# A mixture-of-experts stage: the first expert's first block placed ahead of the turning of the remaining rows

## The chip, the cores and the metric

The kernel runs on one core of one Trainium2 chip. The metric is the device time of one execution in microseconds (us); beside it stands a profile of one execution, taken by the hardware profiler. The engines are named as the profile names them: PE is TensorE (matmuls), PEld its weight loads, DVE is VectorE, ACT is ScalarE, POOL is GpSimd, SP is SyncE, which here only starts DMAs. A name with a q (PEldq, POOLq) is the engine's sequencer, which takes instructions, branches and register loads in order.

## The reference

Two layers of a graph network with attention over 1250 nodes of 512 features (float32), and at the end of the second layer a mixture of eight experts. Only this last part is touched:

```python
def _L1_ffn_ref(x, ln_g, ln_b, w_r, b_r, W1, b1, W2, b2):   # E=8, K=2, 512 -> 2048 -> 512
    h = (x - mu) * jax.lax.rsqrt(var + LN_EPS) * ln_g + ln_b
    logits = jnp.einsum('btd,ed->bte', h, w_r) + b_r
    topk_vals, topk_idx = jax.lax.top_k(logits, K)
    gates = jax.nn.softmax(topk_vals, axis=-1)
    hid = jax.nn.gelu(jnp.einsum('nd,edf->nef', hf, W1) + b1, approximate=False)
    expert_stack = jnp.einsum('nef,efd->ned', hid, W2) + b2
    ...
    mixed = jnp.sum(gathered * gates_flat[:, :, None], axis=1)
    return x + mixed
```

The reference runs every expert on every row and then picks two results per row. The kernel sends each row only to its two experts.

## The kernel before, in words

**Routing and sorting.** The stages ahead of the experts (layer norms, graph sums, attention) work on ten tiles of 125 rows. They leave the normalized rows in DRAM (`rows_d`), and for each row its two experts and its two gates. The 2 x 1250 (row, expert) pairs are sorted by expert into 2500 *slots*: VectorE makes one-hot matrices and TensorE adds them up. The helper `listed` (from line 1157) does this: it makes `blk`, `nblk`, `inb`, then `hotp` and `hotb` for each of the two choices on VectorE, then 20 matmuls into `plist` (line 1179). It is called twice. The first call gives `row_i`, the row of each slot, in 20 *blocks* of 128 slots. The second one gives the lists `to_row` and `to_gate`, the target row and gate of each slot of each block of results; its last copies are lines 1246 to 1254. Between them lie the plan (lines 1203 to 1219) and the gates (from line 1222). The plan has four whole numbers for each expert: its first slot, its number of full blocks of 256, whether what is left of it needs 0, 128 or 192 slots (0, 1 or 2), and its first column in the lists.

**Gathering and turning.** The loop of lines 1191 to 1200 runs over the 20 blocks. GpSimd gathers 128 rows by an indirect DMA (line 1193) into one of five tiles `hg`; TensorE turns the tile by four transposes (line 1197) into a PSUM tile `pg`, of which there are four; `affine_columns` (lines 154 to 163) brings each of the four pieces into `hts`, the rows' features by slots, with scale and shift on the way. VectorE does two of the pieces, ScalarE the other two. `hts` lies in SBUF as a whole.

**Experts.** The loop at the end (lines 1334 to 1346) runs over the eight experts with branches on the plan. First comes what is left over, at one of two widths: `If part > 0` (line 1341), in it `If part == 1` (line 1342), a block of 128, or else of 192. Then `blocks_of_256` (line 1320) follows: up to four ifs, one nested in the other (line 1322), each with a block of 256. A `block` (line 1311) calls `hidden` (line 1260): for each of 16 chunks of the 2048 hidden features four matmuls (line 1266) and one GELU on ScalarE (line 1269). Then `result` (line 1281) has 16 matmuls and one for the bias for each 128 slots (lines 1287 and 1289), and `add_rows` (line 1271) scales by the gate on VectorE (line 1278) and adds the rows to the output in DRAM by an indirect DMA of GpSimd (line 1279). For 192 slots `result_192` (line 1292) does the same turned, with transposes at the end. `plan_of` (line 1326) loads the four numbers of an expert into registers of each engine (line 1328), one expert ahead. With these inputs expert 0 has one block of 128, expert 1 one of 192, expert 2 one of 128; the other five together have four of the small ones and seven of 256.

**Weights.** Each expert has eight tiles of 1 MB (four of W1, four of W2), and 16 places hold two experts. `load_weights` (line 1084) issues them from SP in order, up to a given number. Places 0 to 7 have a pool of their own. Places 8, 9 and 10 lie in `big`, an old buffer of the stages ahead, and places 11 to 15 in a pool `moe_w2` that takes the room of the sorting pools `rt` and `rx`, once nothing uses them any more.

**Order.** Each engine executes its own queue in order. The tile framework's scheduler sets that order by the program's order and the dependences; on SP inside the expert loop the order is that of the program (`manual_schedule`). Between engines semaphores make an instruction wait for its inputs and for the room that it writes.

Of the kernel before, what the change touches and what calls it, by code (L numbers as in the profile page):

```python
# [8 lines left out]
F32 = mybir.dt.float32  # L9
# [10 lines left out]
N = 1250  # L20
# [27 lines left out]
NA_B = (2 * N + E1 * 127) // 128  # L48
WS = 16
# [20 lines left out]
def gps_two_layer_kernel(ctx: ExitStack, tc: tile.TileContext, x, src, dst, ew, rows, cols,  # L70
# [1034 lines left out]
    with tc.tile_pool(name="moe", bufs=1) as ep:  # L1105
# [4 lines left out]
        with tc.tile_pool(name="rt", bufs=1) as rt, tc.tile_pool(name="rx", bufs=3) as rx, \  # L1110
                tc.tile_pool(name="rps", bufs=2, space=PSUM) as ps:
            iota_p = rt.tile([P, 128], F32, name="iota_p")
            nc.gpsimd.iota(iota_p, pattern=[[1, 128]], base=0, channel_multiplier=0,
                           allow_small_or_imprecise_dtypes=True)
            edges_b = rt.tile([P, NB], F32, name="edges_b")
            nc.gpsimd.iota(edges_b, pattern=[[128, NB]], base=0, channel_multiplier=0,
                           allow_small_or_imprecise_dtypes=True)

            tok = rt.tile([P, T, 2], F32, name="tok")
            nc.gpsimd.iota(tok[:, :, 0], pattern=[[0, T]], base=0, channel_multiplier=1,  # L1120
                           allow_small_or_imprecise_dtypes=True)
            nc.gpsimd.iota(tok[:, :, 1], pattern=[[1, T]], base=0, channel_multiplier=0,
                           allow_small_or_imprecise_dtypes=True)
            edges_a = rt.tile([P, NA_B], F32, name="edges_a")
            nc.gpsimd.iota(edges_a, pattern=[[128, NA_B]], base=0, channel_multiplier=0,
                           allow_small_or_imprecise_dtypes=True)
            steps = rt.tile([P, MB], F32, name="steps")
            nc.gpsimd.iota(steps, pattern=[[256, MB]], base=193, channel_multiplier=0,
                           allow_small_or_imprecise_dtypes=True)
            nc.vector.memset(hts[:, :, NB * 128:], 0.0)  # L1130


            prank = ps.tile([P, T, E1], F32, name="prank", tag="pl")
            flat = "p t e -> p (t e)"
            nc.tensor.matmul(prank.rearrange(flat), lower, has.rearrange(flat), start=True, stop=False)
            nc.tensor.matmul(prank.rearrange(flat), ones_b, before[:, :T, :].rearrange(flat), start=False, stop=True)
            pbase = ps.tile([P, E1], F32, name="pbase", tag="pt")
            nc.tensor.matmul(pbase, ones_b, below, start=True, stop=True)
            pcount = ps.tile([P, E1], F32, name="pcount", tag="pt")
            nc.tensor.matmul(pcount, ones_b, before[:, T, :], start=True, stop=True)  # L1140
            base = rt.tile([P, E1], F32, name="base")
            nc.vector.tensor_copy(base, pbase)
            count = rt.tile([P, E1], F32, name="count")
            nc.vector.tensor_copy(count, pcount)


            rank = rt.tile([P, T, E1], F32, name="rank")
            nc.vector.tensor_tensor(rank, prank, base[:, None, :].to_broadcast([P, T, E1]), ALU.add)
            def of_expert(by, name):

                w = rt.tile([P, T, 2, E1], F32, name="hotw", tag="hotw")
                nc.vector.tensor_tensor(w, hot, by, ALU.mult)
                o = rt.tile([P, T, 2], F32, name=name)
                nc.vector.tensor_reduce(o, w, AX.X, ALU.add)
                return o

            def listed(slot, edges, nb, values, nv):

                blk = rt.tile([P, T, 2, nb], F32, name="blk", tag="blk")
                nc.vector.tensor_tensor(blk, slot[:, :, :, None].to_broadcast([P, T, 2, nb]),  # L1160
                                        edges[:, None, None, :].to_broadcast([P, T, 2, nb]), ALU.is_ge)
                nblk = rt.tile([P, T, 2], F32, name="nblk", tag="nblk")
                nc.vector.tensor_reduce(nblk, blk, AX.X, ALU.add)
                inb = rt.tile([P, T, 2], F32, name="inb", tag="inb")
                nc.vector.scalar_tensor_tensor(inb, nblk, -128.0, slot, op0=ALU.mult, op1=ALU.add)
                nc.vector.tensor_scalar(inb, inb, 128.0, None, op0=ALU.add)
                nc.vector.tensor_sub(blk[:, :, :, :nb - 1], blk[:, :, :, :nb - 1], blk[:, :, :, 1:])
                hotp = rt.tile([P, T, 2, 128], BF16, name="hotp", tag="hotp")
                hotb = rt.tile([P, T, 2, nv, nb], BF16, name="hotb", tag=f"hotb{nv}")
                for k in range(2):  # L1170
                    nc.vector.tensor_tensor(hotp[:, :, k, :], inb[:, :, k:k + 1].to_broadcast([P, T, 128]),
                                            iota_p[:, None, :].to_broadcast([P, T, 128]), ALU.is_equal)
                    nc.vector.tensor_tensor(hotb[:, :, k, :, :],
                                            blk[:, :, k, None, :].to_broadcast([P, T, nv, nb]),
                                            values(k)[:, :, :, None].to_broadcast([P, T, nv, nb]), ALU.mult)
                pl = ps.tile([128, nv, nb], F32, name="plist", tag="pl")
                for t in range(T):
                    for k in range(2):
                        nc.tensor.matmul(pl.rearrange("p m b -> p (m b)"), hotp[:, t, k, :],
                                         hotb[:, t, k, :, :].rearrange("p m b -> p (m b)"),  # L1180
                                         start=(t == 0 and k == 0), stop=(t == T - 1 and k == 1))
                return pl

            slot = of_expert(rank[:, :, None, :].to_broadcast([P, T, 2, E1]), "slot")
            plist = listed(slot, edges_b, NB, lambda k: tok, 2)
            row = rt.tile([128, NB], F32, name="row")
            nc.vector.tensor_scalar(row, plist[:, 1, :], float(P), None, op0=ALU.mult)
            nc.vector.tensor_add(row, row, plist[:, 0, :])
            row_i = rt.tile([128, NB], I32, name="row_i")
            nc.vector.tensor_copy(row_i, row)  # L1190
            for b in range(NB):
                hg = rx.tile([128, D], F32, name="hg", bufs=5)
                nc.gpsimd.indirect_dma_start(hg, None, rows_d,
                                             bass.IndirectOffsetOnAxis(ap=row_i[:, b:b + 1], axis=0))
                pt = ps.tile([128, DC, 128], F32, name="pg", tag="pg", bufs=4)
                for c in range(DC):
                    nc.tensor.transpose(pt[:, c, :], hg[:, c * 128:(c + 1) * 128], ident)
                affine_columns(hts[:, :, b * 128:(b + 1) * 128], pt, C_LNG, C_LNB)
# [3 lines left out]
            n256 = rt.tile([P, E1, MB], F32, name="n256")  # L1202
            nc.vector.tensor_tensor(n256, count[:, :, None].to_broadcast([P, E1, MB]),
                                    steps[:, None, :].to_broadcast([P, E1, MB]), ALU.is_ge)
            planf = rt.tile([P, 4, E1], F32, name="planf")
            nc.vector.tensor_copy(planf[:, 0, :], base)
            nc.vector.tensor_reduce(planf[:, 1, :], n256, AX.X, ALU.add)
            nc.vector.scalar_tensor_tensor(planf[:, 2, :], planf[:, 1, :], -256.0, count,
                                           op0=ALU.mult, op1=ALU.add)
            over = rt.tile([P, E1], F32, name="over")  # L1210
            nc.vector.tensor_scalar(over, planf[:, 2, :], 128.0, None, op0=ALU.is_gt)
            nc.vector.scalar_tensor_tensor(planf[:, 2, :], planf[:, 2, :], 0.0, over, op0=ALU.is_gt, op1=ALU.add)
            blocks_of = rt.tile([P, E1], F32, name="blocks_of")
            nc.vector.scalar_tensor_tensor(blocks_of, planf[:, 1, :], 2.0, planf[:, 2, :],
                                           op0=ALU.mult, op1=ALU.add)
            nc.vector.memset(planf[:, 3, 0:1], 0.0)
            for e in range(1, E1):
                nc.vector.tensor_add(planf[:, 3, e:e + 1], planf[:, 3, e - 1:e], blocks_of[:, e - 1:e])
# [175 lines left out]
```

## Time and profile before

| | |
|---|---|
| runs | 1548.17, 1550.3, 1555.47 us; median 1550.3 |
| the profiled execution | 1546.89 us; its span in the profile 1545.2 us, mean clock of TensorE 0.962 |
| TensorE | 5762 matmuls, transposes among them |
| the gathers (line 1193) | 20, starting from 811.3 to 841.2 us |
| result matmuls of line 1287 | 576, 592 ns each |
| hidden matmuls of line 1266 | 1792; 336 to 357 ns each by group |
| weights | 64 tiles of 1024 KB |

The span is what the profile covers from the first to the last instruction; the execution's own time is 1.7 us longer. All positions are us from the start of the span. The expert stage takes the second half, from about 803 us. A line of instructions is read as: start, busy time, engine, line, operation, output <- input, tile and shape, how many, and in brackets the idle time of the engine ahead of it and what ended that. "issue" as a cause of idle time means that the engine waited for nothing that the profile shows; the time then lies in its sequencer. The granted clock is the share of full speed that TensorE's throttle allowed.

### The profile page before, as it was taken

How to read it: one execution, taken by the hardware profiler on the slowest of the kernel's cores; microseconds unless marked ns; L12 is line 12 of the kernel's file. 1: busy time of each engine (PE TensorE's matmuls, PEld its weight loads, DVE VectorE, ACT ScalarE, POOL GpSimd, SP SyncE). 2: the span in 40 equal slices, each digit the busy share in tenths (PEclk: the TensorE clock that was granted, in tenths of full speed). 3: DMA queues.
4: the chain of work that ended last, by engine and by line, in shares of the span. 5: the costliest groups of instructions: out<-in, count | busy, mean ns of one | idle time of the engine just before them, and what ended most of it. 6: DMA issues, size and time to landing. Idle time of an engine off the chain costs nothing. (4 is left out here: it accounts for less than half of the span.)

```text
span 1545.2 us, 17805 instructions
## 1 busy us (share of the span) xinstructions
PE 1424.8 (92%) x5762; PEld 917.7 (59%) x5762; DVE 576.3 (37%) x1424; ACT 405.5 (26%) x937; POOL 95.2 (6%) x90
## 2 busy tenths in 40 slices
PE   6999999999999789999965898898999998899997
PEld 3666666634464436564544596794767567875773
DVE  7767666698876673343476000000000000000000
ACT  9544444400133413111224121210212012120110
POOL 0001100100000000000005000000000000000000
PEclk9999999999999899999985999899999999999999
DMA  7311111442420040001148556600642106000011
GB/s 226 94 53 54 48 54 41 139 129 74 147 75 21 1 157 3 0 0 33 48 154 334 175 187 231 221 9 12 223 139 95 14 8 226 12 6 9 7 14 15
DMA packets 72716, 134.73 MB, mean 87 GB/s; under 512 B 8281, under 2 KB 9673, under 8 KB 72575
## 3 DMA queue, kind: packets, MB, share of 16 engines
q1 hardware_dynamic: 67646, 122.47, 23.5%
q0 software_dynamic: 4928, 10.43, 3.5%
q8 instruction: 82, 1.34, 0.4%
q14 instruction: 60, 0.48, 0.1%
HBM read 107.27 MB, written 26.38 MB: 86 GB/s over the span
## 5 line engine op out<-in xcount | busy, mean ns | idle before, releaser
L1287 PE MATMUL po<-w,big 128*128 128x512 f32 x576 | 250.1, 592 | 0.0
L1266 PE MATMUL pm<-hts,big 128*128 x960 | 186.5, 357 | 21.8 <-issue 21.6
L1266 PEld LDWEIGHTS pm<-hts,big 128*128 128x128 f32 x960 | 168.6, 197 | 41.8 <-issue 26.3
L1278 DVE TENSOR_SCALAR o<-po,to_gate 128x512 f32<-128x512 f32 (+1 forms) x24 | 17.7, 748 | 459.6 <-PE po L1289 458.4
L1287 PEld LDWEIGHTS po<-w,big 128*128 128x128 f32 x576 | 109.1, 190 | 132.1 <-issue 131.5
L1269 ACT ACTIVATE big<-pm,cols_sb 128x256 f32<-128x256 f32 (+2 forms) x224 | 96.4, 432 | 282.2 <-PE pm L1266 281.9
L412 PEld LDWEIGHTS pa<-hm,hs 125*128 125x128 f32 x640 | 106.8, 189 | 95.9 <-issue 69.2
L1266 PE MATMUL pm<-hts,w 128*128 x832 | 144.5, 336 | 18.9 <-DMA big<-in_w_dram 6.0
L1266 PEld LDWEIGHTS pm<-hts,w 128*128 128x128 f32 x832 | 132.9, 197 | 29.8 <-issue 20.6
L412 PE MATMUL pa<-hm,hs 125*128 125x160 f32 x640 | 121.2, 301 | 8.4 <-DVE at L415 7.5
L415 DVE TENSOR_TENSOR at<-at,pa 128x160 f32 x320 | 102.2, 320 | 56.6 <-PE pa L412 33.6
L441 PE MATMUL pm<-big,ht 128*125 128x512 f32 x240 | 123.0, 597 | 0.0
L122 PE MATMUL pm<-w,at 128*125 128x512 f32 x240 | 114.2, 598 | 0.0
L388 ACT ACTIVATE hm<-hm,wt_e 125x80 f32<-125x80 f32 x320 | 86.5, 350 | 84.7 <-DVE hm L385 68.5
L619 PE MATMUL pn<-big,at 125*125 125x512 f32 x200 | 87.8, 596 | 2.1 <-DMA bg_sb<-in_rows_dram 2.1
L441 PE MATMUL pm<-big,xt 128*125 128x512 f32 x160 | 83.8, 612 | 1.2 <-ACT xt L275 1.2
L1269 ACT ACT_TABLE_LOAD x11 | 14.1, 1283 | 267.0 <-PE pm L1266 267.0
L1279 POOL DMA_INDIRECT out_dram<-o,row x24 | 36.9, 1536 | 660.4 <-DVE o L1278 284.4
L619 PEld LDWEIGHTS pn<-big,at 125*125 125x125 f32 x200 | 36.9, 188 | 50.6 <-issue 50.6
L1300 PE MATMUL po<-big,w 128*128 128x192 f32 x384 | 63.9, 327 | 0.0
L1300 PEld LDWEIGHTS po<-big,w 128*128 128x128 f32 x384 | 62.3, 190 | 0.6
L122 PEld LDWEIGHTS pm<-w,at 128*125 128x125 f32 x240 | 41.3, 188 | 34.7 <-issue 34.3
(382 smaller groups left out, 1444.5 us busy)
## 6 DMA issues: line engine op xcount, KB each, us to landing
w<-in_w_dram SPq DMA_DIRECT2D x52, 1024.0 KB
big<-in_w_dram SPq DMA_DIRECT2D x12, 1024.0 KB
x_t<-in_x_dram SPq DMA_DIRECT2D x10, 224.0 KB
xn_d<-xr SPq DMA_DIRECT2D x10, 224.0 KB
y_d<-o SPq DMA_DIRECT2D x10, 224.0 KB
z_d<-o SPq DMA_DIRECT2D x10, 224.0 KB
q_d<-o SPq DMA_DIRECT2D x10, 224.0 KB
k_d<-o SPq DMA_DIRECT2D x10, 224.0 KB
```

The source lines that it names most:

```text
L122: nc.tensor.matmul(ps, lhs[:, c, :], w[:, c, :], start=(c == 0), stop=(row is None and c == DC - 1))
L388: nc.scalar.activation(hm[:, j, 1, :], hm[:, j, 0, :], AF.Copy, scale=wt_e[:, g * J + j:g * J + j + 1])
L412: nc.tensor.matmul(pa.rearrange("p k c -> p (k c)"), hs[:, j, :], hm[:, j, :, :].rearrange("p k c -> p (k c)"), start=True, stop=True)
L415: add = nc.vector.tensor_tensor(to, to, pa.rearrange("p k (t w) -> p k t w", t=T), ALU.add)
L441: nc.tensor.matmul(pm, lhs[:, c, :], w_sb[:, c, :], start=(c == 0), stop=(row is None and c == DC - 1))
L619: nc.tensor.matmul(pn, at[:P, 0, s, t * P:(t + 1) * P], y[:, s, :], start=(s == 0), stop=(s == T - 1))
L1266: nc.tensor.matmul(pm[:, :width], w1s[e, f // DC][:, c, (f % DC) * 128:(f % DC + 1) * 128], hts[:, c, bass.ds(start, width)], start=(c == ...
L1269: nc.scalar.activation(hid[f][:, :width], pm[:, :width], AF.Gelu, bias=cols_sb[:, C_B11 + e * FC + f:C_B11 + e * FC + f + 1])
L1278: nc.vector.tensor_scalar(o[:n], pm[:n], to_gate[:n, here], None, op0=ALU.mult)
L1279: nc.gpsimd.indirect_dma_start(out, bass.IndirectOffsetOnAxis(ap=row[:n], axis=0), o[:n], None, bounds_check=N - 1, oob_is_err=False, comp ...
L1287: nc.tensor.matmul(pm, hid[f][:, s * 128:(s + 1) * 128], w2s[e, f // DC][:, f % DC, :], start=(f == 0), stop=False)
L1300: nc.tensor.matmul(pm[:, :192], w2s[e, f // DC][:, f % DC, chunk], hid[f][:, :192], start=(f == 0), stop=False)
```

## The change

The pieces of the stage are put in another order:

- The plan and both lists (gates too) are made ahead of any turning in the program's text; only the first `HG` = 10 gathers stand ahead of them.
- There are ten tiles `hg` in place of five. They move to the pool `rt`, which stays open until the last row is turned.
- Blocks 0 and 1 of the gathered rows are turned, in PSUM tiles `pg`, and then expert 0's first block runs at once. Its first slot is the constant 0 in place of a register. It is 256 wide if the expert has a full block of 256, or else its leftover at 128 or 192.
- Blocks 2 to 19 are turned behind that block, in the PSUM pool of the results (`po`, four tiles in place of three), with the gathers of blocks 10 to 19 among them, each in the text ahead of the turning of the block eight places before it.
- A new number `left_0` is made on VectorE (three small instructions): expert 0's leftover where it has a full block, else 0. After the turning it is loaded into a register, and the loop over the experts begins for expert 0 with it: its leftover and then its full blocks from the second on. With these inputs both are empty.
- Places 8, 9 and 10 of the weights are asked for by a `load_weights(WS_B)` of their own ahead of the first block. Places 11 to 15 follow, as before, once the sorting pool is closed, which is now behind the turning.

In the instruction order that results, SP issues places 8 and 9 in the routing stage (after the output of its tiles 3 and 7) and 10 ahead of the plan. GpSimd issues twelve gathers, then the row addition of the first block, and then the other eight gathers. TensorE has the list matmuls of the first call, the transposes of blocks 0 and 1, those of the second call, the first block, and then 72 transposes.

```diff
-        with tc.tile_pool(name="rt", bufs=1) as rt, tc.tile_pool(name="rx", bufs=3) as rx, \
-                tc.tile_pool(name="rps", bufs=2, space=PSUM) as ps:
+        left_0 = ep.tile([1, 1], I32, name="left_0")
+        sorting, sums = ExitStack(), ExitStack()
+        rt = sorting.enter_context(tc.tile_pool(name="rt", bufs=1))
+        ps = sums.enter_context(tc.tile_pool(name="rps", bufs=2, space=PSUM))
...
-            for b in range(NB):
-                hg = rx.tile([128, D], F32, name="hg", bufs=5)
-                nc.gpsimd.indirect_dma_start(hg, None, rows_d,
-                                             bass.IndirectOffsetOnAxis(ap=row_i[:, b:b + 1], axis=0))
-                pt = ps.tile([128, DC, 128], F32, name="pg", tag="pg", bufs=4)
-                for c in range(DC):
-                    nc.tensor.transpose(pt[:, c, :], hg[:, c * 128:(c + 1) * 128], ident)
-                affine_columns(hts[:, :, b * 128:(b + 1) * 128], pt, C_LNG, C_LNB)
+        def gather(b):
+            rows_at[b] = rt.tile([128, D], F32, name="hg", bufs=HG)
+            nc.gpsimd.indirect_dma_start(rows_at[b], None, rows_d,
+                                         bass.IndirectOffsetOnAxis(ap=row_i[:, b:b + 1], axis=0))
+        def turn_block(b, psum, **kw):
+            pt = psum.tile([128, DC, 128], F32, **kw)
+            hg = rows_at.pop(b)
+            for c in range(DC):
+                nc.tensor.transpose(pt[:, c, :], hg[:, c * 128:(c + 1) * 128], ident)
+            affine_columns(hts[:, :, b * 128:(b + 1) * 128], pt, C_LNG, C_LNB)
+        for b in range(HG):
+            gather(b)
...
+        nc.vector.tensor_scalar(over[:, 0:1], planf[:, 1, 0:1], 0.0, None, op0=ALU.is_gt)
+        nc.vector.tensor_mul(planf[:, 2, 1:2], planf[:, 2, 0:1], over[:, 0:1])
+        nc.vector.tensor_copy(left_0, planf[0:1, 2, 1:2])
...
+        for b in range(2):
+            turn_block(b, ps, name="pg", tag="pg", bufs=4)
+        sums.close()
+        load_weights(WS_B)
...
             def block(e, plan_e, b, width):
-                start = nc.s_assert_within(first + b * 256, 0, 2 * N - 1, ...)
+                start = 0 if e == 0 and isinstance(b, int) and b == 0 else nc.s_assert_within(...)
...
+            def rest_of(e, plan_e, part, b):
+                with tc.If(part > 0):
+                    with tc.If(part == 1) as one:
+                        block(e, plan_e, b, 128)
+                    with one.Else():
+                        block(e, plan_e, b, 192)
...
-                plans = {0: plan_of(0)}
+                plan_0 = plan_of(0)
+                with tc.If(plan_0[1] > 0) as full_0:
+                    block(0, plan_0, 0, 256)
+                with full_0.Else():
+                    rest_of(0, plan_0, plan_0[2], 0)
+                for b in range(2, NB):
+                    if b + HG - 2 < NB:
+                        gather(b + HG - 2)
+                    turn_block(b, po, name="po")
+                sorting.close()
+                w_pools[1] = ctx.enter_context(tc.tile_pool(name="moe_w2", ...))
+                _, (part_0,) = nc.values_load_multi_w_load_instructions(left_0, min_val=0, max_val=2, ...)
                 for e in range(E1):
                     load_weights(2 * FG * (e + 2))
-                    plan_e = plans.pop(e)
+                    plan_e = plans.pop(e) if e else plan_0
                     if e + 1 < E1:
                         plans[e + 1] = plan_of(e + 1)
-                    with tc.If(plan_e[2] > 0):
-                        with tc.If(plan_e[2] == 1) as one:
-                            block(e, plan_e, plan_e[1], 128)
-                        with one.Else():
-                            block(e, plan_e, plan_e[1], 192)
-                    blocks_of_256(e, plan_e, 0)
+                    rest_of(e, plan_e, plan_e[2] if e else part_0, plan_e[1])
+                    blocks_of_256(e, plan_e, 0 if e else 1)
```

## The prediction

> **What bounds the kernel now.** I read the page first, then the stretch of the trace around the change, since the page averages over very different stages.
>
> ```profile
> PE 1424.8 (92%) x5762; PEld 917.7 (59%) x5762; DVE 576.3 (37%) x1424; ACT 405.5 (26%) x937; POOL 95.2 (6%) x90
> issue 7%; PE 5%; DMA 1%; POOL 0%; DVE 0%; POOLq 0%; DVEq 0%
> ```
>
> TensorE is busy 92% of the span, so only stretches where it idles can give anything. Windows around the expert stage (columns: length, busy time and count of PE, PEld, DVE, ACT, POOL, then granted clock, DMA share, GB/s):
>
> ```profile
> 811.00:851.00 40.00, 22.94 (x100) 15.92 (x100) 24.70 (x64) 15.91 (x40) 21.40 (x20) 0.57 0.87 325
> 851.00:880.00 29.00, 28.49 (x161) 20.39 (x161) 0.38 (x2) 6.94 (x17) 0.00 (x0) 1.00 0.52 184
> 880.00:886.00 6.00, 0.19 (x1) 0.22 (x2) 0.53 (x1) 0.00 (x0) 1.65 (x1) 0.75 0.38 93
> ```
>
> From 811 to 851 rows are gathered and turned and the gate lists made, with TensorE at 0.57 of its clock. From 851 to 880 runs expert 0: one block of 128 slots and nothing else, so the changed program takes the Else path with 128. At 885.8 expert 1 begins. Whatever the change does shows in that last number. The timeline:
>
> ```profile
> 811.32 1.04 POOL L1193 DMA_INDIRECT hg<-rows_d,row_i  x1 [9.42 <-DVE left L1241]
> ...
> 818.36 3.97 PE L1197 MATMUL pg<-ident,hg 128*128 128x128 f32 x16 [8.28 <-DMA hg<-rows_d,row_i]
> ...
> 847.62 2.12 PE L1179 MATMUL plist<-hotb,hotp 125*128 125x162 bf16 x19
> ...
> 851.18 14.54 PE L1266 MATMUL pm<-hts,w 128*128 x128 [1.44 <-DVE to_gate L1254]
> ...
> 879.29 0.38 PE L1289 MATMUL po<-b_parts,row_pick 96*128 96x512 bf16 x1
> ...
> 881.37 1.65 POOL L1279 DMA_INDIRECT out_dram<-o,row  x1 [39.19 <-DMA w<-in_w_dram]
> 885.81 17.82 PE L1266 MATMUL pm<-hts,big 128*128 x96 [6.14 <-issue]
> ```
>
> The first block starts when the last list (to_gate) is ready, 0.25 us after it. Between the experts TensorE idles 6.1 us for "issue", nothing that the timeline shows. The view of the branch lines, by queue, does (ns, one event each; the third is the register load of the next plan):
>
> ```profile
> L1342 PEldq COMPARE_BRANCH  x1: 3397/3397/3397, 872.0 to 872.0; - x1
> ...
> L1322 PEldq COMPARE_BRANCH  x1: 4688/4688/4688, 875.5 to 875.5; - x1
> ...
> L1328 PEldq TENSOR_LOAD <-plan x1: 1002/1002/1002, 880.4 to 880.4; - x1
> ...
> L1342 PEldq COMPARE_BRANCH  x1: 3776/3776/3776, 881.6 to 881.6; - x1
> ...
> L1341 PEldq COMPARE_BRANCH  x1: 3536/3536/3536, 1079.1 to 1079.1; - x1
> ```
>
> A jump over a block that isn't run costs TensorE's sequencer 3.4 to 4.7 us. Two of the three between expert 0 and 1 (872.0, 875.5) lie behind the last result matmuls, since the sequencer runs ahead; the load and the third jump make the 6.1 us.
>
> **The change, part by part** (times of the profiled execution).
>
> *Lists first.* The gather of block 0 starts at 811.4 (one more 0.15 us VectorE operation ahead of it; the two others lie in VectorE's 6.5 us wait for the gather). VectorE takes the first piece of block 0 at 819.5, as now. In the changed instruction order there follow inb, blk, inb (0.8 us), one piece of block 1 (0.4), two hotp of 1.48 and two hotb of 1.83: until 827.6, where before the pieces of eighteen other blocks stood between. The last 19 list matmuls take 2.1 to 2.5, VectorE's six list operations 1.15, and 0.25 as before: the block starts at **831.5 instead of 851.2**. The added jump over the 256 block lies behind this wait, because in the trace the plan's load runs (848.4) while list matmuls are still queued; without that cover the start is 2.9 later.
>
> *The block itself.* 28.5 us now (851.18 to 879.67) at clock 1.00. TensorE will have idled before it, as before expert 2, whose first stage takes 16.45 instead of 14.54: +1.9. It ends at E = **861.9** (879.7 before), 17.8 ahead. W2's tiles, requested by 812, are needed at 848.
>
> *Behind the block: POOL.* GpSimd's queue holds the block's scatter, and in the changed order gathers 12 to 19 stand behind it (0 to 11 are ahead: ten tiles, two freed by the first two turned blocks). So the long idle DMA time of the block carries none of them. Scatter starts at E+1.7 and takes 1.65, then eight gathers 1.25 apart (0.95 + 0.30), the last from E+12.4; its landing is
>
> ```profile
> DMA to landing us min/median/max: 5.4/6.0/6.1
> ```
>
> for the last three of before; with quiet DMA queues I take 5.4: E+17.8. On TensorE 18 blocks take 0.85 each if the clock stays up (ScalarE's two pieces of each block, 0.81, then decide): 15.3; at the half clock 1.25 each as from 826 to 845: 22.5. The clock falls only 3.8 us after the last matmul at 879.7, so the first blocks run at full clock and the gathers decide: last block at **E+17.8 = 879.7**. ScalarE's extra table load (1.28) lies in its 13.6 us idle at the end of the block.
>
> *The jumps behind that.* Here TensorE's sequencer can't run ahead: it waits itself for each gather. After the last one come the load of left_0 (1.0), the jump over expert 0's second pair of blocks (3.5, the row of 1079.1), the jump over its 256 blocks (3.5), the load of plan 1 (1.0), the jump over expert 1's 128 block (3.8), set-up and semaphores 1.1: **13.9**, where before 6.1 showed. Expert 1 starts at 893.6 instead of 885.8: **+7.8**, and all later work moves with it.
>
> *SP's queue.* Two of the weight tiles move from 814 to the routing stage, where the DMA share is 0.28: free. Tiles 11 to 15 (5 MB) need the gather tiles' room and now go out at about 880 instead of 850.8. They took 15 us (851 to 866 at 347 GB/s): landed by 897, needed from 893.6+17.8 = 911. Expert 2's 8 MB behind them are done by about 920, needed at 945. Nothing; with the 15 us margin gone, 1 us for 1.
>
> [...] The rows show 0.07 us where the branch falls through, but 2.2 to 5.8 where it jumps. [...] I take the rows.
>
> **Sum.** Start -19.7, clock +1.9, turning of 18 blocks moved onto the path +17.8, jumps and loads +7.8 (13.9 less 6.1): +7.8. The profiled execution took 1546.9 (span 1545.2 and 1.7 around it), the median of the runs shown is 1550.3, 3.4 above it: forecast 1546.9+7.8 = 1554.7 for such an execution, **1558 as a median**.
>
> **Rivals.**
> 1. *The sequencer runs ahead past the turned blocks* (not slower). Where the last gathers land before TensorE has worked off the queued transposes, the load and the first two jumps are hidden as at 872 to 880, and 13.9 falls to 6.1: 1550. For it: turning at the half clock is slower than the gathers, which gives up to 4 us of queue. Against: before, each block's transposes follow its own landing. It decides only from 8 us of queued work; four PSUM tiles hold about 5.
> 2. [...] All 18 blocks at 1.25 (+4.7), and the three jumps meet the 5 MB of weights at full DMA load, 4.7 each instead of 3.6 (+3.3): +16, 1566. For it: the clock of 0.5 through 826 to 847 in the same kind of work, jumps of 4.6 to 5.8 in other places.
> 3. *Expert 1's weights come late*: if SP asks 15 us later than I think, or the DMA gives half its rate, w1's last tile stalls about 10 to 15 us: 1570.
>
> That the block still waits for all rows can be left out: its matmuls read fixed columns, and their waits name only the first two blocks' writers.
>
> **How the numbers follow.** What a measurement can tell from no change is 0.5%, 7.8 us, just where the forecast lies. Forecast 0.55 (own range 1554 to 1562, half of it above the bound), rival 1 0.17, rival 2 0.20, rival 3 0.05, something that makes it faster 0.03. Slower: 0.29+0.20+0.05 = 0.54; same 0.41; faster 0.05 (0.02 from rival 1). The range 1551 to 1567 takes in rivals 1 and 2 but for their ends.
>
> **What would show it.** The first block's start near 831.5 and its end near 862; gathers 12 to 19 starting 3.6 us after it, 1.25 apart; the last transposes near 880; two long TensorE branches with no work over them and expert 1 near 894. An expert 1 before 886 makes the sum wrong; a stall inside its first stage means rival 3.

## The result, and the profile after

The changed kernel takes 1559.76 us (median of 8 runs, 1555.28 to 1562.26), the kernel before 1551.61 (8 runs): a ratio of 1.0047, 95% interval 1.0029 to 1.0066. The profiled executions, both at the fast end of their runs, have spans of 1553.6 and 1545.2 us, 8.4 apart. The forecast was 7.8.

The engines' busy time on the page of the changed kernel:

```profile
PE 1419.0 (91%) x5762; PEld 913.9 (59%) x5762; DVE 576.9 (37%) x1427; ACT 406.2 (26%) x938; POOL 94.5 (6%) x90
```

TensorE does the same 5762 pieces of work in 5.8 us less busy time, in a span that is 8.4 longer: it waits more. Where is read from windows cut at the ends of the steps (length, busy and count of PE, PEld, DVE, ACT, POOL, then granted clock, DMA share, GB/s):

```profile
811.00:832.50 21.50, 5.45 (x34) 4.09 (x30) 13.32 (x42) 1.72 (x4) 13.41 (x12) 0.50 1.04 386
832.50:862.80 30.30, 30.26 (x163) 22.47 (x164) 0.15 (x1) 8.45 (x18) 0.00 (x0) 0.94 0.09 31
862.80:879.60 16.80, 11.84 (x73) 7.98 (x71) 12.32 (x34) 12.26 (x33) 9.33 (x9) 0.93 0.48 134
879.60:898.10 18.50, 0.00 (x0) 0.00 (x0) 1.44 (x5) 1.41 (x4) 0.00 (x0) 0.50 0.84 292
```

The first row is gathering and lists, the second expert 0's block, the third the turning of blocks 2 to 19. In the fourth, 18.5 us long, TensorE does nothing and VectorE and ScalarE work for 1.4 us each: only the DMA queues are busy, at 292 GB/s. The second row shows the reverse, 30 us in which TensorE is full and the DMA queues are all but idle. The timeline of the changed kernel:

```profile
832.54 16.34 PE L1285 MATMUL pm<-hts,w 128*128 128x128 f32 x128 [1.50 <-DVE to_gate L1270]
...
862.45 0.38 PE L1308 MATMUL po<-b_parts,row_pick 96*128 96x512 bf16 x1
...
863.97 1.65 POOL L1298 DMA_INDIRECT out_dram<-o,row  x1 [34.89 <-DVE o L1297]
...
865.93 1.00 POOL L1198 DMA_INDIRECT hg<-rows_d,row_i  x1 [0.30 <-issue]
...
874.79 0.95 POOL L1198 DMA_INDIRECT hg<-rows_d,row_i  x1 [0.30 <-issue]
...
877.37 2.19 PE L1205 MATMUL po<-ident,hg 128*128 128x128 f32 x8 [0.64 <-DMA hg<-rows_d,row_i]
...
879.64 0.38 SPq L1099 DMA_DIRECT2D w<-in_w_dram  x1
880.08 5.91 SPq L1102 DMA_DIRECT2D w<-in_w_dram  x4
...
898.18 17.31 PE L1285 MATMUL pm<-hts,big 128*128 x96 [18.62 <-issue]
```

The block starts and ends early, then eight gathers follow its row addition, the last transposes end at 879.56, and expert 1 waits for "issue". At 879.6 SP asks for the 5 MB that need the sorting pool's room. The branch lines, by queue (ns; only those of TensorE's sequencer are shown):

```profile
L1375 PEldq TENSOR_LOAD <-left x1: 318/318/318, 878.5 to 878.5; - x1
...
L1356 PEldq COMPARE_BRANCH  x2: 82/1756/3431, 878.9 to 891.5; - x2
...
L1342 PEldq COMPARE_BRANCH  x1: 7636/7636/7636, 882.6 to 882.6; - x1
...
L1348 PEldq TENSOR_LOAD <-plan x1: 996/996/996, 890.4 to 890.4; - x1
...
L1357 PEldq COMPARE_BRANCH  x1: 6133/6133/6133, 891.6 to 891.6; - x1
```

The jump at 878.9 (over expert 0's empty leftover) takes 3.43 us; it began ahead of the weights. The two jumps during the weights take 7.64 and 6.13. The second event of line 1356 (891.5, 0.08 us) falls through. The load of left_0 and the first 0.6 us of the first jump lie beside the last transposes; what is left of these lines makes 17.6 of the 18.6 us.

| step | before, us | after, us | difference | forecast |
|---|---|---|---|---|
| end of the first list's matmuls (work ahead of the change) | 810.08 | 811.17 | +1.1 | 0 |
| from there to expert 0's block | 41.10 | 21.37 | -19.7 | -19.7 |
| the block | 28.49 | 30.29 | +1.8 | +1.9 |
| turning behind it | none | 16.73 | +16.7 | +17.8 |
| from there to expert 1 | 6.14 | 18.62 | +12.5 | +7.8 |
| expert 1 to the end of the span | 659.4 | 655.4 | -4.0 | 0 |
| sum | | | +8.4 | +7.8 |

The sum came out by luck, from two errors that cancel: the gap ahead of expert 1 is 4.7 us longer than forecast, and 4.0 us came back later, which the forecast didn't have.

### The profile page after: what moved, and what is told of

The parts are those of the page before. It is cut to its first block, busy times and chain, and to the rows that moved or that the text cites. A ratio compares the mean times of both kernels' runs of the same rounds, so it can differ in the third digit from the quotient of the medians.

```text
span 1553.6 us, 17732 instructions
## 1 busy us (share of the span) xinstructions
PE 1419.0 (91%) x5762; PEld 913.9 (59%) x5762; DVE 576.9 (37%) x1427; ACT 406.2 (26%) x938; POOL 94.5 (6%) x90
## 5 line engine op out<-in xcount | busy, mean ns | idle before, releaser
L1285 PE MATMUL pm<-hts,w 128*128 (+1 forms) x832 | 146.8, 339 | 15.6 <-PEq L1356 5.9
```

The lines of the kernel that those rows point to most:

```text
L1285: nc.tensor.matmul(pm[:, :width], w1s[e, f // DC][:, c, (f % DC) * 128:(f % DC + 1) * 128], hts[:, c, bass.ds(start, width)], start=(c == ...
```

## The experiments

All ratios below are to runs of the kernel before on the same chip. In traces, "gap" is TensorE's idle time from the last matmul or transpose to expert 1's first matmul.

**Without the second pair (a_no_rest).** `rest_of` and `blocks_of_256` are not built for expert 0 behind the turning, and left_0 isn't loaded.

```diff
-                    rest_of(e, plan_e, plan_e[2] if e else part_0, plan_e[1])
-                    blocks_of_256(e, plan_e, 0 if e else 1)
+                    if e:
+                        rest_of(e, plan_e, plan_e[2], plan_e[1])
+                        blocks_of_256(e, plan_e, 0)
```

> Leaves out expert 0's further blocks (its second leftover and its full blocks from the second on), which are empty with these inputs. Theory J (TensorE's sequencer stands in jumps that nothing covers, each 3.4 us on quiet DMA queues and 6 to 8 under the weights): behind the last transposes only the plan's load (1.0) and one jump (about 6) remain, expert 1 starts about 8.5 us after them instead of 18.6, and the time falls by 10 to about 1550. Rival G (the gathers and the turning on the path are what costs, the sequencer would only stand somewhere else): the gap stays above 15 and the time stays within 3 us of 1559.8.

Measured 1547.26 us, ratio 0.9977 (0.9966 to 0.9989): two jumps fewer turn the loss into a small gain. Its timeline:

```profile
882.83 0.37 SPq L1099 DMA_DIRECT2D w<-in_w_dram  x1
...
887.06 17.63 PE L1285 MATMUL pm<-hts,big 128*128 x96 [4.32 <-issue]
```

and the line of its one jump:

```profile
L1357 PEldq COMPARE_BRANCH  x1: 3794/3794/3794, 882.9 to 882.9; - x1
```

The gap is 4.3, not 8.5: the jump began at 882.9, 0.1 us after SP's first request for weights, and took 3.8, though the DMA share over it was 0.68, and the plan's load lay beside the last transposes. Rival G falls: gathers and turning stand here as in the changed kernel (16.8 us behind the block), and the time is below that of before. From expert 1 on the two kernels take the same, 655.9 and 655.4 us, so what the edit moves behind it isn't the reason.

**Later weights (d_late_weights).** Six memsets of place 11 on GpSimd stand ahead of its load.

```diff
+            if i == WS_B:
+                for _ in range(6):
+                    nc.gpsimd.memset(a, 0.0)
```

> The changed kernel, with weight places 11 to 15 asked for later: six memsets of GpSimd on place 11 stand ahead of the load, so the 5 MB start some 10 us later and the DMA queues are quiet during the jumps. Theory J with fetches slowed by the weights: the jumps of 7.6 and 6.1 fall to 3.4 to 4.7, expert 1 starts 4 to 5 us earlier (about 14 after the last transposes instead of 18.6), time 1555. Rival L (the length of a jump has to do with its place or with chance, not with the DMA load): jumps stay at 6 to 8 and the time at 1560, or above, if expert 1's weights then come late.

Measured 1552.77 us, ratio 1.0007 (0.9996 to 1.0018), so 7 below the changed kernel, of which the gap makes 4.7. The memsets in its timeline, then its gap and its second jump in the view of windows, then the three jumps in the view of the branch lines:

```profile
881.19 11.11 POOL L1095 MEMSET w<- 128x2048 f32 x6 [3.62 <-PE po L1208]
892.33 0.38 SPq L1102 DMA_DIRECT2D w<-in_w_dram  x1
```

```profile
881.00:895.00 14.00, 0.12 (x2) 0.07 (x1) 1.44 (x5) 1.39 (x4) 10.82 (x6) 0.54 0.15 33
...
884.73:889.53 4.80, 0.00 (x0) 0.00 (x0) 0.00 (x0) 0.00 (x0) 4.63 (x4) 0.50 0.05 9
```

```profile
L1359 PEldq COMPARE_BRANCH  x1: 3631/3631/3631, 880.9 to 880.9; - x1
...
L1345 PEldq COMPARE_BRANCH  x1: 4796/4796/4796, 884.7 to 884.7; - x1
...
L1360 PEldq COMPARE_BRANCH  x1: 3573/3573/3573, 891.0 to 891.0; - x1
```

Asking for the same 5 MB 11.3 us after the last transposes instead of 0.1 takes the DMA share in the gap from 0.84 to 0.15, the two jumps from 7.64 and 6.13 to 4.80 and 3.57, and the gap from 18.6 to 13.9. Expert 1 doesn't wait for the later weights. Rival L falls for these jumps.

The 4.80 is not DMA load: the share during that jump is 0.05. It begins 0.2 us after the end of another jump. That goes together in all fourteen traces: from 800 us on, at a DMA share of at most 0.15, the 22 jumps that come less than 1 us behind another one take 4.57 to 5.06 us and the 103 others 3.28 to 3.95 (jumps below 1 us left out). Why isn't shown.

**All rows turned first, branches of the change (c_turn_before), and of before (b_lists_first).** Both make both lists first and turn all 20 blocks ahead of expert 0; b has the branches of before.

```diff
-        for b in range(2):
+        for b in range(NB):
             turn_block(b, ps, name="pg", tag="pg", bufs=4)
+            if b + HG < NB:
+                gather(b + HG)
```

> Only the order of the lists is changed: both lists first, ten gather tiles, but all 20 blocks turned ahead of expert 0, with the branches of before. Theory J: no branch is added, so the gap ahead of expert 1 stays at about 6 us; the turning still ends near 848 to 851, bound by gathers and TensorE at half clock, so the first block starts 0 to 3 us earlier than 851.2 and the time is 1549 to 1552. Rival G': lists first is itself a loss (VectorE's list work delays the turning): the first block starts after 853, and the time is 1554 or more.

> As the kernel with lists first and all rows turned ahead of expert 0, but with the branches of the changed kernel: first block, then left_0 and the second, empty pair. Theory J: the sequencer runs about 7.7 us ahead of TensorE at the end of a block, so what comes first is covered and only the added jump (3.4) and load (0.3 to 1.0) show: gap ahead of expert 1 about 10 us instead of 6, time 4 us above the kernel with lists first only. If a jump in itself cost more than its own fetch, or if all jumps were uncovered, the gap would be 14 or more; if all were covered, 6.

Lists first alone: 1547.79 us, ratio 0.9977 (0.9963 to 0.9991), 1.2 us below the range expected (1549 to 1552). The first block came 33.9 us after the first list, not 38 to 41: eighteen turned blocks cost only 12.5 us ahead of the block (33.9 less the changed kernel's 21.4), where behind it they cost 16.7. With the added branches: 1554.35, ratio 1.0020 (1.0004 to 1.0037), 6.6 above b where 4 was expected. The gap was 11.8 against 6.5, 5.3 more where 4 was expected, since the added jump, right behind another, took 4.57. More came from a place that I had taken as covered, the jump over expert 0's 256 block. Its line, then the window around it:

```profile
L1369 PEldq COMPARE_BRANCH  x1: 6853/6853/6853, 848.8 to 848.8; - x1
```

```profile
847.70:856.30 8.60, 0.04 (x1) 0.07 (x1) 1.29 (x4) 1.72 (x5) 0.00 (x0) 0.71 0.83 303
```

Here places 11 to 15 come in just then, at 303 GB/s, and the jump of 6.9 us holds up the first block: it starts 40.1 us after the first list instead of 33.9. In the changed kernel the same jump took 0.35, at a DMA share of 0.94, so load alone doesn't make a jump long. In the two profiles 9.4 us of all this come back from expert 1 on (655.8 us to the end instead of 665.2), so the 6.6 are a net figure and no measure of one jump.

**One outer branch (e_one_if).** left_0 gets a second number, the count of expert 0's further blocks, and one `If` on it encloses the second pair.

```diff
...
+                        with tc.If(more_0 > 0):
+                            rest_of(0, plan_0, part_0, plan_0[1])
+                            blocks_of_256(0, plan_0, 1)
```

> Expert 0's second pair stands in one outer branch on a count made beside left_0 (nothing of the computation is left out): TensorE's sequencer jumps once in place of twice. Theory J: the gap between the last transposes and expert 1 falls from 18.6 us by one jump under the weights (6 to 7.6) to about 12 (0.4 load, 3.5 and 6 of jumps, 1.0 load, 1.1), time about 1553. Rival W (the gap is set by expert 1's weights, and jumps only fill it): the gap stays within 2 us of 18.6 and the time at 1559.

Measured 1553.43 us, ratio 1.0015 (1.0002 to 1.0027); the gap is 11.7. Its two jumps, the first ahead of the weights and the second among them:

```profile
L1387 PEldq COMPARE_BRANCH  x1: 3607/3607/3607, 884.9 to 884.9; - x1
```

```profile
L1358 PEldq COMPARE_BRANCH  x1: 6996/6996/6996, 889.9 to 889.9; - x1
```

One jump fewer is 6.9 us less gap and 6.3 us less time. Rival W falls: expert 1 starts 11.6 us after SP's first request for these weights where the changed kernel has 18.5. (The turning behind the block took 18.8 us in this profile instead of 16.7, so counted from the block's end expert 1 comes only 4.9 earlier.)

**More gathers ahead of the row addition (f_twelve).** Twelve tiles `hg`, and six blocks turned ahead of the block, four of them by ScalarE alone.

```diff
-HG = 10
+HG = 12
+EARLY = 6
...
+        for b in range(2, EARLY):
+            turn_block(b, ps, True, name="pg", tag="pg", bufs=4)   # True: ScalarE takes all four pieces
```

> The changed kernel with twelve gather tiles and six blocks turned ahead of the first block (blocks 2 to 5 by ScalarE alone), so that 18 gathers stand ahead of the first block's row addition on GpSimd and two behind it; branches as in the changed kernel. Theory Q (behind the block the eight gathers, which stand behind the row addition, set the end of the turning): the last transposes come 11 us after the block's end instead of 16.7, expert 1 starts 5.5 us earlier, time about 1554. Rival P (TensorE's and ScalarE's own turning time sets it, or the early pieces on ScalarE hold up the block): the turning still ends 15 or more after the block, or the block starts 3 or more later, and the time stays at 1558 to 1561.

Measured 1556.76 us, ratio 1.0034 (1.0024 to 1.0043): 3 less than the changed kernel, where 5.8 was expected, and the intervals of the two ratios overlap. The turning behind the block shrank as theory Q says, from 16.7 to 9.9 us. But nothing of it reached expert 1, which starts 86.8 us after the first list where the changed kernel has 87.0: the block started 23.0 after the list instead of 21.4, took 4.0 longer, 2.5 of them in a stop after six matmuls, and the gap was 1.0 longer. The timeline of this kernel:

```profile
833.10 1.62 PE L1289 MATMUL pm<-hts,w 128*128 128x128 f32 x6 [1.50 <-DVE to_gate L1277]
...
837.24 1.01 PE L1289 MATMUL pm<-hts,w 128*128 128x128 f32 x4 [2.52 <-issue]
```

The stop of 2.5 us is for "issue", with gathers and weights at a DMA share of 0.98 from 831 to 838. The same stop is in both kernels built on it below and not in the changed kernel. That the six more gathers are its cause is likely and not shown.

**All parts together (v1_all, v2_loads).** Twelve tiles, one outer branch, four memsets ahead of place 11, TensorE's order by the program's text, and the loads of left_0 and of the next plan ahead of the first block (v1) or right behind it (v2):

```diff
+                _, (part_0, more_0) = nc.values_load_multi_w_load_instructions(left_0, ...)
+                plans[1] = plan_of(1)
                 for b in range(EARLY, NB):
```

> Both together, with the register loads of left_0 and of the next plan ahead of the first block, and the 5 MB of weights held back by four memsets on GpSimd (7.4 us). Theories J and Q: last transposes 11 us after the block, then two jumps on quiet queues (3.5 and 3.6) and 1.1: expert 1 starts about 19.5 us after the end of the block where the changed kernel has 35.3; time about 1544, 7 to 8 below the kernel before. If jumps or gathers were not what holds it, 1553 or more.

> As the kernel with all parts together, but the register loads of left_0 and of the next plan stand behind the first block instead of ahead of it, where TensorE's sequencer runs ahead of its matmuls. Theory J: the 1.6 us that these loads cost ahead of the first block go and come back nowhere, the first block starts 1.5 us earlier against the lists, time about 1546. If the sequencer had no lead there, the loads would show behind the block and the time stays at 1547.7.

v1 took 1547.67 us, ratio 0.9971 (0.9960 to 0.9981), v2 1546.65, ratio 0.9978 (0.9968 to 0.9989): both faster than before by a quarter of a per cent, less than expected, and no different from each other. From the block's end to expert 1 v1 needs 18.6 us where the changed kernel needs 35.4; 19.5 was expected. What was missed lies ahead: the block starts 24.0 us after the first list and stops for 2.6 us as in f_twelve. In v2 it still starts 23.7 after the first list, so the loads cost 0.3, not 1.6.

**The 4 us that came back (b_pad, b_pad_again, b_pad_128, h_before_pad).** The jump ahead of expert 6 took 3.52 us before and 0.45 in the changed kernel. Nothing of the change touches expert 6, but its code lies elsewhere in TensorE's instruction stream. To test this, lists first only got a block that no data can reach, at the end of a path that these inputs jump over anyway:

```diff
                     with one.Else():
                         block(e, plan_e, b, 192)
+                        if e == 0:
+                            with tc.If(plan_e[1] > MB - 1):
+                                block(0, plan_e, 0, 256)      # 128 in b_pad_128
```

> The kernel with lists first only, with a block of 256 that no data can reach put at the end of expert 0's 192 path, which these inputs jump over anyway: no jump is added, only the code behind it moves. Theory C (whether a short jump stalls depends on where its target lies in the fetched code, so code position alone gives or takes about 3 us at expert 6, where the changed kernel's jump took 0.45 and that of before 3.5): the jump ahead of expert 6 changes from 3.5 to below 0.5 and the time falls by 3 to about 1545. Rival N (chance of the run, or the DMA load, decides): the jump stays at 3.5 and the time at 1548.

> The kernel before with the same unreachable block of 256 at the end of expert 0's 192 path; nothing else changed. Theory C (code position alone): the jump ahead of expert 6 falls from 3.5 to below 0.5 us as in the kernel with lists first and the pad, and the time falls by 3 to 10 us; lists first then gives 2 to 5 beside it. Rival S (the gain of the padded kernel comes from its earlier first block together with luck of that run): the jump stays at 3.5 and the time within 2 us of the kernel before.

> The kernel with lists first and the unreachable block of 256, unchanged, on the chip of the next run. Theory C: its time is a property of its code, 1537 to 1541. Rival S (luck of the earlier run): 1545 to 1549, as lists first without the block.

> The same with an unreachable block of 128 instead of 256: the code behind it lies about 35 instructions further forward. Theory C: the stalls at experts 4 and 6 are those of this position, and the time stands apart from the padded kernel (1538.3) or the kernel without pad (1547.8) only as far as these stalls differ: if the jump of expert 6 is short and no stall lies in expert 4's first matmuls, about 1538 to 1541; if both stall, 1545 to 1549. Rival N (the pad does something else): time and stalls do not go together.

Measured: 1538.30 us, ratio 0.9931 (0.9912 to 0.9951), 9.5 below lists first where 3 was expected, and in the second trial on another chip 1545.65, ratio 0.9965 (0.9944 to 0.9986). By its time that second trial falls to rival S: the ratio is no longer apart from that of lists first without the block. With a block of 128 1550.54, ratio 0.9998 (0.9982 to 1.0013). The kernel before with the same 256 block 1554.20, ratio 1.0022 (1.0009 to 1.0035). The jump ahead of expert 6 in the kernel before, in the changed kernel, in lists first, in b_pad and in b_pad_128:

```profile
L1342 PEldq COMPARE_BRANCH  x1: 3516/3516/3516, 1285.0 to 1285.0; - x1
```

```profile
L1357 PEldq COMPARE_BRANCH  x1: 448/448/448, 1295.4 to 1295.4; - x1
```

```profile
L1361 PEldq COMPARE_BRANCH  x1: 3941/3941/3941, 1286.3 to 1286.3; - x1
```

```profile
L1361 PEldq COMPARE_BRANCH  x1: 441/441/441, 1280.6 to 1280.6; - x1
```

```profile
L1361 PEldq COMPARE_BRANCH  x1: 3721/3721/3721, 1289.6 to 1289.6; - x1
```

| kernel | jump ahead of expert 6 | pauses inside experts 3 and 4 | TensorE idle in all | at half clock | expert 1's first to the last matmul |
|---|---|---|---|---|---|
| before | 3.52 | 1.28 | 33.0 | 41.6 | 651.0 |
| changed | 0.45 | none | 31.4 | 33.7 | 646.9 |
| lists first | 3.94 | 3.11 | 35.0 | 50.2 | 656.3 |
| lists first, 256 | 0.44 | none | 29.2 | 32.1 | 644.4 |
| the same again | 0.44 | none | 29.3 | 28.2 | 644.0 |
| lists first, 128 | 3.72 | 2.05 | 33.2 | 39.1 | 651.7 |
| before, 256 | 3.41 | 4.23 | 35.6 | 44.9 | 654.1 |

All columns are in us; the last three are of the stretch from expert 1's first to the last matmul. The code of experts 1 to 7 does the same work in every row. Behind a pause came slow work: in each trace, every time that TensorE falls idle for 5 us or more from expert 1 on, a stretch at a granted clock of 0.5 begins 2.0 to 5.3 us after its last matmul, and in lists first and in the kernel before with 256 the further pause in expert 4 goes with a stretch of 13.7 us instead of 3.4 to 6.8. Around the start of expert 4, in lists first and in b_pad:

```profile
1072.00:1092.00 20.00, 10.61 (x33) 8.38 (x32) 1.06 (x3) 2.70 (x4) 1.54 (x1) 0.66 0.88 300
```

```profile
1074.00:1094.00 20.00, 14.12 (x59) 12.22 (x60) 0.99 (x3) 4.33 (x8) 1.54 (x1) 0.83 0.89 302
```

Of the 11.9 us between lists first and the padded kernel half is idle time (35.0 against 29.2); the other half is slower work, with 50 us at half clock against 32. One code gives the same jump, no pause and the same 644 us in a profile on each of two chips; moving it by some instructions gives 652. So for lists first the jump and the pauses go with where the code lies. How much of the 11.9 us does so is open: every other row is one profile, and the twelve executions of lists first alone run from 1540.4 to 1553.3 us, with mean clocks from 0.969 to 0.959.

Theory C as it was written for h_before_pad fell: the same block put into the kernel before left the jump at 3.41 and the time rose by 3.7, which rival S didn't expect either. Which positions are short, and by what rule, isn't shown. In the two profiles of b_pad the first block started 33.8 us after the first list on one chip and 38.8 on the other, with two pauses of 2.2 us in the turning; b_pad_128, on that second chip, has the same two pauses. Their cause is open, and so is most of the 7 us between the two medians, since the spans of the two profiled executions are only 2.7 us apart.

## Why the prediction was right, and where it was not

- **Lists first: right to 0.1 us.** The block came 19.7 earlier. The jump over the 256 block cost nothing there, but by luck: it took 0.35, and c_turn_before shows the same jump at 6.85 and uncovered.
- **The block and the clock: right.** +1.8 against +1.9. The clock in the turning was 0.93, so the half-clock part of rival 2 fell. (Before, the clock fell 3.3 us after the last matmul at 879.7, not 3.8.)
- **GpSimd's queue: right, the size in part by luck.** Gathers 12 to 19 started 3.1 us after the block's end, some 1.27 apart, and set the end of the turning: 16.7 for 17.8. f_twelve confirms that they do. But they landed 3.5 to 4.2 us after their issue, not 5.4, and the last block's own transposes (1.1 us at half clock), which the sum left out, came on top.
- **The jumps: the mechanism right, the size wrong.** "the jump over expert 0's second pair of blocks (3.5 ...), the jump over its 256 blocks (3.5) ... the jump over expert 1's 128 block (3.8)" were 3.43, 7.64 and 6.13, 17.2 together instead of 10.8. The two loads were 0.32 and 1.00 instead of 2.0. With the weights out of the way (d_late_weights) the jumps still make 12.0: for the second one, right behind another, the prediction took 3.5, though its own row of 875.5, also a jump over expert 0's 256 blocks right behind another one, had 4.69. The other 5.2 are the weights. The gap of d_late_weights, 13.9 as forecast, comes out because the loads and the set-up were taken too long. a_no_rest and e_one_if show that the jumps cause the loss, d_late_weights that the weights make them longer.
- **SP's queue: right on the wait, wrong on "Nothing".** No weight came late. But the 5 MB that the change moves to 880 fill the DMA queues in just the time in which TensorE jumps: 4.7 us of gap, and so the whole miss in that term. Rival 2 had this at 4.7 us a jump and a chance of 0.20; the step should have been in the forecast.
- **What a jump costs: right in kind, too low.** "The rows show 0.07 us where the branch falls through, but 2.2 to 5.8 where it jumps": in the changed kernel the branch at 891.5 that falls through took 0.08, and two of the three jumps ahead of expert 1, 7.64 and 6.13, lie above that range. That the code behind a jump is fetched, as the expectations of c_turn_before, d_late_weights and b_pad have it, was my own assumption: no trace here shows a fetch, only jumps of 17.2 us together under the weights and of 12.0 without them.
- **Rival 1 fell.** The load of left_0 began at 878.49, with the last block's transposes (from 878.47): TensorE's sequencer was 1.1 us ahead and not the 8 that the rival needs.
- **"all later work moves with it": wrong by 4.0 us.** In the profiles 6.5 us come back in two places, expert 3's first block (a pause of 1.28 gone, and less half clock behind it) and the jump ahead of expert 6; other places take 2.4. That this is the position of the code is likely from b_pad, and not shown for this kernel.

The change moved 18 blocks of turning from ahead of the block, where they cost 12.5 us with the lists out of the way, to behind it, where they cost 16.7, and paid two jumps for it. TensorE's own time for these 72 transposes is 12.4 us ahead of the block and 12.0 behind it. What the change gained it gained by making the lists first, and that alone is 0.23% faster than before.

## What to carry to other kernels

Here a taken branch on TensorE mostly cost 3.3 to 4 us on quiet DMA queues (0.45 ahead of expert 6 in the changed kernel), 4.6 to 5.1 directly behind another one, and up to 7.7 under a bulk load, unless the sequencer had queued matmuls to hide it (7.7 us of them at the end of expert 0's block before). So put work that makes the sequencer wait (gathers, PSUM to be freed: behind them, in the changed kernel, it was 1.1 us ahead) ahead of a long block rather than between a block and the next branch, keep two branches from following each other uncovered, and don't let a bulk load start there. When work is moved, ask whether it overlaps something in the new place. With code moved, a later jump took another time here (0.44 us in lists first with the 256 block, 3.94 without it), so judge a small change by the trace of its own stage and not by the total alone.

## What the hardware showed that I had not expected

- Two things go with the length of a jump. One is DMA load: the same three jumps took 3.63, 4.80 and 3.57 us at DMA shares of 0.03, 0.05 and 0.32 (d_late_weights), and 3.43, 7.64 and 6.13 at 0.40, 1.03 and 0.66 (the changed kernel). The other is a jump just ahead of it: 4.57 to 5.06 us instead of 3.28 to 3.95 at a share of at most 0.15.
- Three times in this study a block's first matmuls stopped for 2.5 to 2.6 us with no wait that the profile shows (f_twelve, v1_all, v2_loads), at a DMA share of 0.89 to 0.98.
- A register load on TensorE's sequencer took 0.32 us for one number, 0.56 to 0.59 for two, 1.0 for four, though up to 1.78 in some places.
- The jump ahead of expert 6 took 0.44 or 0.45 us in some kernels and 3.4 to 3.9 in others, and in lists first an unreachable block in front of it changed that from 3.94 to 0.44.
- Slow work followed the pauses of TensorE: with each one of 5 us or more from expert 1 on went a stretch of 3.4 to 13.7 us at a granted clock of 0.5.
